# Masked queries on GpSimd in the first attention, and another order of work at the start of the second attention and in the tail

## The chip, the cores and the metric

The kernel runs on one core of one Trainium2 chip, all in fp32. The metric is the device time of one execution in microseconds. The kernel before took 1477.64 us, the median of three runs (1471.13 to 1481.87).

## What is computed

The state x has 64 batch items of 128 rows and 128 features. Two blocks follow each other, each an attention and a feed-forward layer with experts:

```python
x = x + xattn0(layernorm(x), fside, ctx, ctx)        # keys: 128 made from fside, 120 given by ctx
x = x + ffn0(layernorm(x))                           # top 2 of 8 experts, 352 wide, SiLU gate
x = x + xattn1(layernorm(x), ctx, ctx)               # keys: 120 made from ctx
x = x + ffn1(layernorm(x))                           # top 2 of 8 experts of rank 64, GELU, factor 2
```

Both attentions have 16 heads of 8 features: `softmax(q k^T / sqrt(8)) v`, then an output projection with a bias. `q = xn wq + bq`; keys and values are made likewise, and in the first attention the raw context rows are appended to both.

## The kernel before

**Tiling.** A group is four batch items (GB = 4, 16 groups), and an iteration is one item. Groups and items are numbered from 0. With heads of only eight features, the 128 rows of a transposed query tile hold all 16 heads, and a score product uses a strip of 32 rows (`ra`, four of them). To keep the heads that share a strip apart, the query tile is made four times (NS = 4 slots s), each with all features but those of its heads set to zero. That is `q4`, 128 x (4 items, 4 slots, 128 queries). The zeroing is done with a column of `hmask` (128 x 4), the slot's own. In the first attention the scores are taken twice: with queries as rows, to get each row's largest score (`max_bank`, matmul L394, VectorE's reduction L414), and with keys as rows, to get the exponentials in the layout that the product with the values needs (`score_bank`, L430, ScalarE's exp L438). The largest scores are put into unused rows of `q4` by `shift` (transposes L459, VectorE L462), so that L430 subtracts them by itself. In the second attention the largest scores come from an unmasked query tile `qf` (L295) and masked keys `k4`, which `prep_heads` makes with four VectorE multiplications (L313); matmul L407.

**The loop** (L554 on). Iteration `it` takes the largest scores of item `it`, the exponentials of `it - 2`, the product with the values of `it - 3` (L475, `out1` L484), and the output projection of `it - 4` and `it - 5` (L495 to L516). All PSUM tiles are taken from one pool of eight banks (`mtile`, L276). In between, `prep(it, half)` makes what the next group needs, one piece at a time: with j = it % 4, the first attention makes queries at j = 0 (`prep_q`), values and keys at j = 2, and at j = 3 the transposed normed rows `xnT` of the group after it (`prep_x`: four transposes L176 and ScalarE's copy L177). `xnT` has one buffer. `prep_q` is a matmul L292 into a bank, and then ScalarE makes two slots in each half of the iteration: four ACTIVATE L301 a group, each with the slot's column of `bq` as bias and of `hmask` as scale. Group 0 of the first attention is made item by item in `prep_batch`.

**Order.** The code runs under a manual schedule: TensorE, ScalarE, VectorE and GpSimd execute their instructions in the order in which the program issues them, and each waits at the head of its order. GpSimd has the norm of each group (L138 to L146 for mean and root, L167 for the normed rows), the residual's bias (L526), the router's work, and the scatters.

**The router** (class at L625) works on items behind the attention, while it goes on. It is made of generators with due times; `call` is made twice an iteration and takes the pieces that are due: the norm and the logits of a group (`front`; transposes L176, copy L177, products L681), the selection of the two experts of two groups at once (`back`: in the first layer GpSimd's L761, L764, L769 and VectorE's L763 and L768, then in both layers VectorE's small operations on 128x64 elements L718 to L735, and the rows' places L858 to L861), and `sent`, which hands rows out by an indirect transfer from GpSimd (L807) behind a copy of one element (L806) that paces it.

**The second layer.** The experts of the second layer run beside the second attention, in pieces (`Aside1.experts`): the transposed gates (L1420), the first product (L1427) with GELU, the gates spread over the hidden rows (L1439, VectorE L1444), the second product (L1450). `Aside1.rest` (L1469) runs what is left when the attention has ended: one piece, then three router calls, and so on. L740 and L741 are the last operations of the selection, on VectorE and ScalarE.

**Start of the second attention.** Ahead of its loop, the kernel makes the transposed rows (`prep_x(0)`), masked keys (`prep_heads(0)`) and queries (`prep_q(0, 0)`, `prep_q(0, 1)`) of group 0. Group 1 is made in iterations 0 and 1: keys (`prep_k`: matmul L202, ScalarE's L207 twice) and values and rows in 0, queries and masked keys in 1. `loads(1)` issues the transfer of group 1's context rows (L256) just before.

Of the kernel before, what the change touches and what calls it, by code (L numbers as in the profile page):

```python
# [8 lines left out]
F32 = mybir.dt.float32  # L9
I32 = mybir.dt.int32  # L10
AF = mybir.ActivationFunctionType
ALU = mybir.AluOpType
# [6 lines left out]
GB = 4  # L19
NG = B // GB  # L20
S = 128
D = 128
# [22 lines left out]
def transformer_kernel(ctx, tc, a, out):  # L45
    nc = tc.nc
# [185 lines left out]
    def attention(layer, w, norm, first, aside):  # L232
# [5 lines left out]
        with ExitStack() as es:  # L238
# [50 lines left out]
            def prep_q(g, v):  # L289
                if v == 0:  # L290
                    pqs[g] = mtile()
                    nc.tensor.matmul(pqs[g], lhsT=w["wq"], rhs=xnTs[g], start=True, stop=True)  # L292
                pq = pqs[g]
                if v == 0 and not first:
                    nc.scalar.activation(  # L295
                        qfs[g], pq.rearrange("p (b q) -> p b q", b=GB), AF.Identity,
                        bias=w["bqf"],
                    )
                for i in range(2):
                    s = 2 * v + i  # L300
                    nc.scalar.activation(  # L301
                        q4s[g][:, :, s, :], pq.rearrange("p (b q) -> p b q", b=GB),
                        AF.Identity, bias=w["bq"][:, s : s + 1], scale=hmask[:, s : s + 1],
                    )

            def prep_k(g):
                keys_of(w, src[g], g, n0, mtile())

            def prep_heads(g):

                k4s[g] = work.tile([128, NS, GB, KC], F32, name="k4", tag="k4")
                for s in range(NS):
                    nc.vector.tensor_scalar(  # L313
                        k4s[g][:, s], k2[g % 2][:, s // 2], hmask[:, s : s + 1], None, ALU.mult
                    )
# [23 lines left out]
            def prep(it, half):  # L339

                g, j = it // GB + 1, it % GB
                if not first:
                    if g == 1:
                        if (j, half) == (0, 0):
                            prep_k(1)
                            prep_v(1)
                        elif (j, half) == (0, 1):
                            prep_x(1)
                        elif j == 1:
                            prep_q(1, half)  # L350
                            if half:
                                prep_heads(1)
                    elif g < NG:
                        pieces = (
                            (), (lambda: prep_k(g),),
                            (lambda: (prep_heads(g), prep_v(g)), lambda: prep_x(g)),
                            (lambda: prep_q(g, 0), lambda: prep_q(g, 1)),
                        )[j]
                        if half < len(pieces):
                            pieces[half]()  # L360
                    return
                if half == 0 and it < GB - 1:
                    prep_batch(it + 1)
                if (it, half) == (0, 1):
                    prep_v(0)
                    norm_of(1)
                if (it, half) == (1, 1):
                    biased(0)
                if (it, half) == (2, 1):
                    prep_x(1)  # L370
                if (it, half) == (3, 0):
                    prep_q(1, 0)
                    prep_q(1, 1)
                if (j, half) == (3, 1):
                    if g + 1 < NG:
                        prep_x(g + 1)
                elif g >= NG:
                    return
                elif j == 0 and it:
                    prep_q(g, half)  # L380
                elif (j, half) == (2, 0):
                    prep_v(g)
                elif (j, half) == (2, 1):
                    prep_k(g)
# [145 lines left out]
            if first:  # L530
                loads(0)
                yield
                context_k(0)
                yield
                context_v(0)
                loads(1)
                yield
                prep_k(0)
                prep_batch(0)
                yield  # L540
            else:

                ps_[0] = work.tile([128, nc_, 4, 512], F32, name="p", tag="p")
                loads(1)
                for g in range(2):
                    normed[g] = READY[g]
                prep_x(0)
                prep_heads(0)
                prep_q(0, 0)
                prep_q(0, 1)  # L550
            oTs, pos_ = {}, {}
# [745 lines left out]
    aside0 = Aside0()  # L1297
    steps = attention(0, l0, norms[0], True, aside0)
    next(steps)
    l0.update(attention_weights("a0_", ("wq", "bq")))  # L1300
    hmask = load_const("hmask", [128, NS], a["hmask"])
    next(steps)
    l0.update(attention_weights("a0_", ("wv", "bv")))
# [41 lines left out]
    class Aside1:  # L1345
# [122 lines left out]

        def rest(self, mtile):  # L1469
            self.mtile = mtile  # L1470
            while next(self.work, self) is not self:
                for _ in range(3):
                    self.router.call(None, mtile)

    with ExitStack() as es:
# [6 lines left out]
def _laid_out(inp):  # L1482

    import numpy as np

    A = {k: np.asarray(v) for k, v in inp.items()}

    def moved(w):
        w = w.reshape(-1, NV, 4, 2 * HD)[:, ::-1]
        return w.transpose(0, 2, 1, 3).reshape(-1, D)  # L1490

    heads = np.arange(D).reshape(4, NV, 2, HD)
    hm, km, sm = (np.zeros((D, n), np.float32) for n in (NS, NV, NV))
    for v in range(NV):
        km[heads[:, 1 - v].ravel(), v] = 1.0
        sm[np.arange(4) * 32 + 16 * v, v] = 1.0
        for i in range(2):
            hm[heads[:, 1 - v, i].ravel(), 2 * v + i] = 1.0

    o = {"x": A["x"]}  # L1500
    o["fsideT"] = A["fside_BxSxS_0"].transpose(2, 0, 1)
    c = A["ctx_1024"]
    o["ctxT"] = c.transpose(2, 0, 1)
    k = moved(c.reshape(B * KC, D)).reshape(B, KC, 1, D)
    o["ctx_k"] = np.where(km.T > 0, k, sm.T).transpose(3, 2, 0, 1)
    v = np.zeros((B, KC, H // 2, 2, 32), np.float32)
    for i in range(2):
        v[:, :, :, i, 16 * i : 16 * i + HD] = c.reshape(B, KC, H // 2, 2, HD)[:, :, :, i]
        v[:, :, :, i, 16 * i + HD] = 1.0
    o["ctx_v"] = v.reshape(B, KC, H * 32).transpose(1, 0, 2)  # L1510
    o["hmask"], o["kmask"], o["smask"] = hm, km, sm
    for p, l, names, tr in (
        ("a0_", "L0_xattn_", ("Wq", "bq", "Wk", "bk", "Wv", "bv", "Wp", "bp"), False),
        ("a1_", "L1_xattn_", ("W_q", "b_q", "W_k", "b_k", "W_v", "b_v", "W_o", "b_o"), True),
    ):
        wq, bq, wk, bk, wv, bv, wo, bo = (A[l + n] for n in names)
        if tr:
            wq, wk, wv, wo = wq.T, wk.T, wv.T, wo.T
        o[p + "wq"], o[p + "wk"] = moved(wq), moved(wk)
        o[p + "bq"] = np.where(hm > 0, moved(bq).T, np.float32(0.0))  # L1520
        if tr:
            o[p + "bqf"] = moved(bq).T
        o[p + "bk"] = np.where(km > 0, moved(bk).T, sm)
        o[p + "wv"], o[p + "bv"] = wv, bv
        o[p + "wo"], o[p + "bo"] = wo, bo
    o["wqkvT"] = A["L0_ffn_wqkv"].T

    w1 = np.zeros((E, D, 2, NF * 128), np.float32)
    w1[..., :F] = A["L0_ffn_w1"].reshape(E, 2, F, D).transpose(0, 3, 1, 2)
    w2 = np.zeros((E, NF * 128, D), np.float32)  # L1530
    w2[:, :F] = A["L0_ffn_w2"].transpose(0, 2, 1)
    w12 = np.concatenate(
        [w1.reshape(E, D, 2, NF, 128).transpose(0, 1, 3, 2, 4).reshape(E, D, NF, 256),
         w2.reshape(E, NF, 128, D).transpose(0, 2, 1, 3)], axis=3,
    )
    o["w12"] = w12.reshape(E, D, NF * 384)
    o["upper"] = np.triu(np.ones((128, 128), np.float32), 1)
    o["ones"] = np.ones((128, 128), np.float32)
    o["steps256"] = np.arange(CAP // TT, dtype=np.float32) * TT

    t = np.zeros((4, 32, 4, 2, 64), np.float32)
    for e in range(E):
        t[:, e, e // 2, e % 2, :] = 1.0
    o["select"] = t.reshape(128, 4, 128)
    o["tiles"] = np.arange(NA, dtype=np.float32).reshape(1, -1)
    o["row_number"] = np.arange(1, 129, dtype=np.float32).reshape(-1, 1)
    o["first_row"] = np.arange(E, dtype=np.float32) * CAP
    o["wgT"] = A["L1_ffn_Wg"].T
    o["bg"] = A["L1_ffn_bg"]
    o["lw1T"] = A["L1_ffn_W1"].transpose(2, 0, 1).reshape(D, E * R)  # L1550
    o["lw2T"] = A["L1_ffn_W2"].transpose(0, 2, 1).reshape(E * R, D)
    return {k: np.ascontiguousarray(v) for k, v in o.items()}
# [18 lines left out]
```

## Time and profile before

The table is of one profiled execution.

| what | us |
|---|---|
| median of three runs | 1477.64 |
| the profiled execution's own time | 1476.76 |
| its span (first to last instruction) | 1474.9 |
| first attention, loop in its steady part: 60 to 600 us, TensorE busy | 531.13 of 540 |
| routed tiles of the first layer: 600 to 940 us, TensorE busy | 325.86 of 340 |
| start of the second attention: 940 to 1050 us, TensorE busy | 100.61 of 110 |
| second attention, 1050 to 1400 us, TensorE busy | 334.81 of 350 |
| tail, 1400 to 1475 us, TensorE busy | 61.72 of 75 |
| granted TensorE clock, mean over the span | 0.987 of full speed |

How to read the profile: PE is TensorE (PEld its loading of weights), DVE is VectorE, ACT is ScalarE, POOL is GpSimd, SP the engine whose queue issues most transfers; L301 is line 301 of the kernel before. A row of the timeline has its start, its length, engine, line, operation, `output<-inputs` with the tiles' names, and in brackets how long the engine was idle before it and whose result ended that. A row with xN stands for N like instructions close to each other. A row of groups has count, total busy time, mean ns of one, and idle time with its releaser. Ends of matmuls are modelled, so a wait of TensorE inside a stretch can read as busy.

### The profile page before, as it was taken

To read this page: it belongs to the slowest core of one execution; us is meant where nothing else is said; L and a number is where in the kernel's file an instruction comes from. 1 tells how busy PE (TensorE), PEld (TensorE's weight loads), DVE (VectorE), ACT (ScalarE), POOL (GpSimd) and SP (SyncE) were. 2 spreads that over 40 slices of the span, in tenths; PEclk is the share of its full clock that TensorE was granted. 3 is DMA by queue.
4 is the path that set the end of the run, shared out by engine and by line. 5 is a ranking of instruction groups with operands and counts; after the bars stand their busy time and mean duration, and the time that the engine had idled before them with its cause. 6 is when DMAs were issued, how large, how long until landed. Compare 5 with 4: busy or idle time off the path is not lost.

```text
span 1474.9 us, 42033 instructions
## 1 busy us (share of the span) xinstructions
PE 1403.5 (95%) x16620; PEld 1099.4 (75%) x16620; DVE 1111.6 (75%) x3025; ACT 845.2 (57%) x1759; POOL 647.0 (44%) x1195
## 2 busy tenths in 40 slices
PE   7999999999999999999999999898999999999987
PEld 5677777777777777788899998576677677767765
DVE  6777888888888888646574444588988878888863
ACT  3666666666666656643333333466766666766644
POOL 4123346565656554665100131557655666554210
PEclk9999999999999999999999999899999999999999
DMA  8422223333222213247777777301111111110000
GB/s 205 120 77 76 77 77 90 88 92 89 76 64 65 64 44 79 85 141 212 227 215 210 209 215 214 94 28 33 33 30 37 30 40 37 33 30 23 9 16 22
DMA packets 143718, 133.02 MB, mean 90 GB/s; under 512 B 48546, under 2 KB 126114, under 8 KB 141602
## 3 DMA queue, kind: packets, MB, share of 16 engines
q1 hardware_dynamic: 135330, 113.02, 27.9%
q0 software_dynamic: 8192, 17.32, 3.8%
q8 instruction: 132, 2.16, 0.6%
q14 instruction: 64, 0.52, 0.1%
HBM read 97.32 MB, written 32.97 MB: 88 GB/s over the span
## 4 chain that ended last, share of the span: by engine, by line
PE 75%; DVE 17%; POOL 4%; issue 2%; DMA 1%; ACT 1%; SPq 1%; POOLq 0%; DVEq 0%; ACTq 0%
PE bank L430 11%; PE bank L1115 11%; PE bank L394 10%; PE bank L475 9%; DVE nm L414 6%; PE bank L1128 5%; PE bank L1427 4%; PE bank L1450 4%; DVE q L462 2%; PE bank L407 2%; PE bank L214 2%; PE bank L511 2%; PE bank L681 2%; PE bank L202 2%; PE bank L176 2%; PE bank L292 2%
## 5 line engine op out<-in xcount | busy, mean ns | idle before, releaser
L414 DVE TENSOR_REDUCE nm<-bank 128x2 f32<-128x496 f32 (+1 forms) x768 | 463.5, 663 | 82.3 <-PE bank L430 63.2
L438 ACT ACTIVATE p<-bank 120x512 f32<-120x512 f32 (+1 forms) x768 | 402.3, 605 | 130.1 <-PE bank L430 128.4
L430 PE MATMUL bank<-q,k 32*120 32x256 f32 (+1 forms) x3072 | 438.8, 399 | 12.3 <-DVE q L462 5.4
L430 PEld LDWEIGHTS bank<-q,k 32*120 32x120 f32 (+1 forms) x3072 | 294.0, 181 | 51.5 <-DVE nm L414 17.5
L394 PE MATMUL bank<-k,q 32*128 32x248 f32 x2048 | 291.6, 400 | 0.7 <-ACT q L334 0.5
L394 PEld LDWEIGHTS bank<-k,q 32*128 32x128 f32 x2048 | 202.8, 189 | 47.8 <-issue 10.9
L1119 ACT ACTIVATE p<-bank 128x256 f32<-128x256 f32 x213 | 81.0, 384 | 189.3 <-PE bank L1115 189.2
L475 PE MATMUL bank<-p,v 128*32 128x128 f32 (+1 forms) x4096 | 176.2, 276 | 0.3
L1120 DVE TENSOR_TENSOR p<-p,bank 128x256 f32<-128x256 f32 x213 | 86.5, 419 | 89.0 <-ACT p L1119 88.4
L407 PE MATMUL bank<-k,qf 32*128 32x480 f32 x512 | 146.6, 604 | 0.8 <-ACT qf L295 0.8
L807 POOL DMA_INDIRECT xs<-xn,at x128 | 129.6, 1013 | 27.8 <-issue 24.3
L484 ACT COPY ov<-bank 128x256 f32<-128x256 f32 x128 | 48.1, 376 | 142.9 <-PE bank L475 142.9
L475 PEld LDWEIGHTS bank<-p,v 128*32 128x32 f32 (+1 forms) x4096 | 109.3, 110 | 22.7 <-issue 13.8
L1115 PE MATMUL bank<-q 128*128 128x256 f32 x516 | 119.0, 380 | 5.2 <-DMA q<-in_w 3.4
L1367 POOL DMA_INDIRECT yb<-ys,back x112 | 109.0, 973 | 27.7 <-issue 20.9
L167 POOL TENSOR_SCALAR xn<-x,mv,rstd 128x128 f32<-128x128 f32 x252 | 114.3, 465 | 7.1 <-issue 1.0
L462 DVE SCALAR_TENSOR_TENSOR q<-bank,c_smask,q 128x256 f32<-128x256 f32 x256 | 111.1, 476 | 7.2 <-PE bank L459 7.0
L1115 PEld LDWEIGHTS bank<-q 128*128 128x128 f32 x516 | 94.8, 190 | 17.5 <-issue 4.3
L475 PE MATMUL bank<-p,vc 120*32 120x128 f32 x2048 | 103.2, 272 | 0.0
L301 ACT ACTIVATE q<-bank,c_a_bq,c_hmask 128x512 f32<-128x512 f32 x124 | 90.1, 789 | 9.8 <-PE bank L292 9.8
L1157 POOL DMA_INDIRECT kvT<-ys,back x16 | 15.4, 963 | 175.5 <-PE bank L1128 106.4
L138 POOL TENSOR_TENSOR mv<-st 128x4 f32<-128x4 f32 x31 | 6.4, 207 | 196.0 <-DVE st L109 196.0
(227 smaller groups left out, 2469.5 us busy)
## 6 DMA issues: line engine op xcount, KB each, us to landing
q<-in_w SPq DMA_DIRECT2D x43, 576.0 KB, 3.8
vc<-in_w SPq DMA_DIRECT2D x28, 576.0 KB
vc<-in_ctx_v SPq DMA_DIRECT2D x16, 960.0 KB, 7.0
ys<-zero SPq DMA_DIRECT2D x71, 128.0 KB, 1.9
k<-in_ctx_k SPq DMA_DIRECT2D x32, 240.0 KB, 2.8
q<-xs SPq DMA_DIRECT2D x43, 128.0 KB, 2.1
ys<-q SPq DMA_DIRECT2D x43, 128.0 KB, 2.9
x<-in_x SPq DMA_DIRECT2D x16, 256.0 KB, 4.4
```

Source lines behind the costliest of these rows:

```text
L167: nc.gpsimd.tensor_scalar(xn[:, j, :D], xg[g][:, j, :], self.mv[:, b, 0:1], self.rstd[:, b : b + 1], ALU.add, ALU.mult,)
L301: nc.scalar.activation(q4s[g][:, :, s, :], pq.rearrange("p (b q) -> p b q", b=GB), AF.Identity, bias=w["bq"][:, s : s + 1], scale=hmask[:, ...
L394: nc.tensor.matmul(pa[:, u, :], lhsT=q4s[g][r, j, s, :], rhs=k2[g % 2][r, s // 2, j, :], start=True, stop=True,)
L407: lambda: nc.tensor.matmul(pa, lhsT=qfs[g][r, j, :], rhs=k4s[g][r, :, j, :], start=True, stop=True),
L414: nc.vector.tensor_reduce(nm[b % 2].rearrange("q i (a s) -> q a i s", s=16)[:, 2 * ra + v : 2 * ra + v + len(slots) // 2, :, 0], pa.rearra ...
L430: nc.tensor.matmul(pb[:n, v * 256 : (v + 1) * 256], lhsT=k2[g % 2][r, v, j, k0 : k0 + n], rhs=q4s[g][r, j, 2 * v : 2 * v + 2, :].rearrange ...
L438: nc.scalar.activation(ps_[b][:n, c, ra, :], pb[:n], AF.Exp, scale=SCALE)
L462: nc.vector.scalar_tensor_tensor(q, pm, smask[:, v : v + 1], q, ALU.mult, ALU.add)
L475: nc.tensor.matmul(pav[32 * ra : 32 * ra + 32, v * S : (v + 1) * S], lhsT=vs[g % 2][c][:, j, 4 * v + ra, i, :], rhs=p[:n, c, ra, (2 * v + ...
L807: s = nc.gpsimd.indirect_dma_start(xs, bass.IndirectOffsetOnAxis(at[:, j, k : k + 1], 0), xn, None)
L1115: nc.tensor.matmul(ph[:, u, :], lhsT=w[:, c, u * 128 : (u + 1) * 128], rhs=xT, start=True, stop=True)
L1367: nc.gpsimd.indirect_dma_start(y[:, k, b % 2, :], None, ys, bass.IndirectOffsetOnAxis(back[:, b, k : k + 1], 0),)
```

## The change

First attention: for groups 1 to 15, ScalarE makes one unmasked tile of queries with the plain bias `bqf`, and GpSimd makes the four slots from it, two in each call of `prep_q`. The tile takes the buffer of the tag "xnT". `bqf` (128 x 1) is loaded for the first layer too. In the order of the built program, GpSimd's four multiplications follow the scatters of the iteration with j = 0 directly and stand ahead of L138 of the next.

Second attention: the keys of group 1 are made ahead of the loop, before the queries of group 0, and its masked keys in iteration 2 instead of 1; in the built order these four L313 stand behind the VectorE part of `shift` of one item and ahead of the next one's. One exp of a constant is written ahead of all this; it depends on nothing, and in the built program it is ScalarE's first instruction of all.

Tail: the first two pieces in `rest` are followed by no router calls. TensorE's order there becomes L1420, L1427, L1439 of group 13, then L176 and L681 of group 15, then L1450 of group 13.

Lines behind the first edit move by 10 to 15: L313 becomes L323, L394 L404, L414 L424, L430 L440, L438 L448, L475 L485, and so on.

```diff
@@ prep_q
+                if first:
+
+                    if v == 0:
+                        qfs[g] = work.tile([D, GB * S], F32, name="xnT", tag="xnT", bufs=1)
+                        nc.scalar.activation(qfs[g], pq, AF.Identity, bias=w["bqf"])
+                    for s in range(2 * v, 2 * v + 2):
+                        nc.gpsimd.tensor_scalar(
+                            q4s[g][:, :, s, :], qfs[g].rearrange("p (b q) -> p b q", b=GB),
+                            hmask[:, s : s + 1], None, ALU.mult,
+                        )
+                    return
                 for i in range(2):
@@ prep
                         if (j, half) == (0, 0):
-                            prep_k(1)
                             prep_v(1)
                         elif (j, half) == (0, 1):
                             prep_x(1)
                         elif j == 1:
                             prep_q(1, half)
-                            if half:
-                                prep_heads(1)
+                        elif (j, half) == (2, 0):
+                            prep_heads(1)
@@ attention, ahead of the second attention's loop
+                nc.scalar.activation(again[:, 1:2], again[:, 0:1], AF.Exp)
...
                 prep_heads(0)
+                prep_k(1)
                 prep_q(0, 0)
                 prep_q(0, 1)
@@ loading
-    l0.update(attention_weights("a0_", ("wq", "bq")))
+    l0.update(attention_weights("a0_", ("wq", "bq", "bqf")))
@@ Aside1.rest
+            n = 0
             while next(self.work, self) is not self:
-                for _ in range(3):
+
+                n += 1
+                for _ in range(3 if n > 2 else 0):
                     self.router.call(None, mtile)
@@ the host's layout
-        if tr:
-            o[p + "bqf"] = moved(bq).T
+        o[p + "bqf"] = moved(bq).T
```

## The prediction, written before the changed kernel was run

> **What bounds the kernel now.** I read the page from the top: busy time, the chain that ended last, then the group of instructions that the change removes.
>
> ```profile
> PE 1403.5 (95%) x16620; PEld 1099.4 (75%) x16620; DVE 1111.6 (75%) x3025; ACT 845.2 (57%) x1759; POOL 647.0 (44%) x1195
> ...
> PE 75%; DVE 17%; POOL 4%; issue 2%; DMA 1%; ACT 1%; SPq 1%; POOLq 0%; DVEq 0%; ACTq 0%
> ...
> L301 ACT ACTIVATE q<-bank,c_a_bq,c_hmask 128x512 f32<-128x512 f32 x124 | 90.1, 789 | 9.8 <-PE bank L292 9.8
> ```
>
> TensorE is busy 95% of the span, and three quarters of the chain run over it; ScalarE is 57% busy and holds 1% of the chain. By these averages nothing is to be had from ScalarE. The average hides that the first attention has four kinds of iteration, so the next view is the table by stretches, cut at the first `values` matmul (L475) of an iteration: one that makes queries (j = 0), its successor (j = 1), and iteration 60, also j = 0, but with no group left to make queries for.
>
> ```profile
> core 0: us, PE busy (x) PEld busy (x) DVE busy (x) ACT busy (x) POOL busy (x), PEclk, DMA share, GB/s
> 197.12:207.50 10.38, 10.07 (x143) 7.10 (x142) 8.85 (x25) 7.72 (x15) 4.28 (x13) 1.00 0.09 27
> 207.50:216.25 8.75, 8.75 (x144) 7.08 (x143) 7.41 (x22) 5.15 (x11) 6.60 (x17) 1.00 0.35 101
> 575.16:583.35 8.19, 8.19 (x140) 6.56 (x139) 7.99 (x23) 4.95 (x11) 5.65 (x16) 1.00 0.00 0
> ```
>
> Without queries the iteration takes 8.19 us; with them 10.38. The one matmul that is added (L292) runs 1.06. So 10.38 - 8.19 - 1.06 = 1.13 us are a wait, although PE's row reads as busy (ends of matmuls are modelled). Cross-check: j = 1 is 8.75 with four transposes (0.44) that a bare iteration lacks, so 8.31 bare, close to 8.19. VectorE is not the cause: j = 0 keeps its length at 7.7 to 9.2 us of VectorE work. ScalarE has 7.72 us of work, and in ScalarE's timeline two L301 stand ahead of the four exps (L438) of each half:
>
> ```profile
> 200.18 1.45 ACT L301 ACTIVATE q<-bank,c_a_bq,c_hmask 128x512 f32<-128x512 f32 x2 [0.66 <-PE bank L292]
> 201.52 2.29 ACT L438 ACTIVATE p<-bank 120x512 f32<-120x512 f32 x4
> ```
>
> The exps run back to back behind them, up to 1.45 us after their scores, and they free the PSUM banks that TensorE fills next. The second pair of L301 follows at 203.84, and its matmul's result keeps one of eight PSUM banks from 200.2 to 205.3.
>
> **Part 1, masked queries (first attention, groups 1 to 15).** Removed: four L301 a group (784 ns each); added: one ACTIVATE with one pointer (the second attention's L295, the same shape, 690 ns), four GpSimd multiplications. The bank is free after one instruction. Gain: 1.13 us in 14 groups (2 to 15), less 0.3 since iteration 52 has 10.27 us of VectorE work in 11.29: 14 x 1.1 - 0.3 = -15.1 us. Group 1 is made in iteration 3 with GpSimd idle; there the copy L177 of the next group must wait until the four are done with the shared buffer, about when it ran before: 0.
>
> The cost is on GpSimd. The trace has no 128x512 tensor_scalar there. Its nearest row:
>
> ```profile
> L167 POOL TENSOR_SCALAR xn<-x,mv,rstd 128x128 f32<-128x128 f32 x252 | 114.3, 465 | 7.1 <-issue 1.0
> ```
>
> Call one operation x. The timeline sets L167 432 ns apart, and the tensor_scalars of 128x4 (L142 to L144, 199 ns each) 260 ns: 172 ns for 124 more elements, 1.39 ns each, x = 0.26 + 508 x 0.00139 = 0.97. By recorded durations (199 to 451 median) x = 1.24; by straight proportion to L167, 4 x 0.43 = 1.73, an end I give little. Here a rule speaks: the Trainium skill, "GPSIMD Engine Reference", section 3.1 Elementwise, gives 1.8 cycles an element as a good loop with one input (769 ns for 512 elements) and 1.03 as the floor for two operations or fewer, which with the 0.2 us that the small rows cost is an estimated 0.65. L167 at 1.39 ns an element is slower than both. I take 0.90, between 0.97 and the 0.77 of the page, nearer the row; 0.65 and 1.24 stay as ends.
>
> What queues behind them: the four sit in GpSimd's order behind the two scatters of j = 0 and ahead of the norm chain (L138 and on) of j = 1. GpSimd delays TensorE in two ways.
> (a) The port. This trace shows VectorE held up beside GpSimd:
>
> ```profile
> 1024.66 2.68 DVE L313 TENSOR_SCALAR k<-k,c_hmask 128x480 f32<-128x480 f32 x4
> ...
> 1025.76 1.31 POOL L526 TENSOR_TENSOR x<-x,c_a_bo 128x512 f32<-128x512 f32 x1
> ```
>
> The four L313 take 1.60 elsewhere; here one waits about 1 us for the end of L526. VectorE operations that read PSUM (L414, L462) keep their times. That is the rule of the skill's "SBUF — State Buffer", section Who interferes with whom: VectorE's two-input SBUF operations, and its copies and tensor_scalars there, share a port pair with GpSimd exclusively. By the row alone only L313 would be hit, which the first attention has not, and the price would be nothing; by the rule the router's small operations are hit too, and I take the rule. In even groups (iterations 25, 33 .. 57, five of them) the four start at 243.75, and VectorE's L718 to L734 come due at 245.98 - 1.1 = 244.88: 4x - 1.1 us late; then L414, which has 0.77 us to spare, and about 0.3 overlaps with what needs no port: 4x - 2.2 lost. In odd ones (29, 37, 45, 53) the pair L858/L861 meets them the same way.
> (b) Lateness. In odd groups L761 stands behind the norm chain:
>
> ```profile
> 283.85 0.21 POOL L138 TENSOR_TENSOR mv<-st 128x4 f32<-128x4 f32 x1 [2.35 <-DVE st L109]
> ...
> 292.65 1.07 POOL L761 TENSOR_TENSOR pp<-lg 128x512 f32<-128x512 f32 x1
> ...
> 294.92 0.68 DVE L763 TENSOR_REDUCE r<-pp 128x64 f32<-128x512 f32 x1
> ```
>
> GpSimd idles 2.35 us before L138, and L763 starts 1.2 after L761 ends (293.72), so the four may cost 3.55 - 1.1; past that L763 waits, L414 behind it on VectorE, and TensorE for that: 4x - 2.45, not on top of the port's loss in the same group but instead of it. So nine groups lose 4x - 2.2: at 0.90, 9 x 1.4 = +12.6; at 0.65 +3.6; at 1.24 +24.8.
>
> **Part 2, keys of group 1 in the second attention's preamble.** The key matmul L202 is put ahead of the queries' L292, which before ran at 939.73. The keys' transfer is issued at 939.03 and such ones take 2.7 us: L202 runs at 941.5 and L292, L295 and the first scores come up to 1.2 us later. Against that, the four L313 leave this place:
>
> ```profile
> 952.32 1.60 DVE L313 TENSOR_SCALAR k<-k,c_hmask 128x480 f32<-128x480 f32 x4
> ...
> 954.37 0.47 PE L430 MATMUL bank<-q,k 32*120 32x256 f32 x1 [2.06 <-DVE q L462]
> ```
>
> They stood ahead of L462, for which TensorE waits 2.06; L430 gains 1.6 and has lost 1.2. But its exp must load a table first (1.28, at 954.52) and stands behind four L301 that are 1.2 late. Net +1.0 (-0.5 to +2.5). The extra exp written there stands as ScalarE's first instruction of the program, with the table load that came first anyway, and the load at 954.52 stays: 0. The added 128x1 constant delays hmask and the first context keys by about 0.5 us on SP's queue; the keys land near 8 and are needed at 10.6: 0.
>
> **Part 3, tail.** TensorE idles in the last router call:
>
> ```profile
> 1436.54 0.33 PE L176 MATMUL bank<-ident,xn 128*128 128x128 f32 x1 [3.14 <-POOL xn L167]
> ```
>
> Group 13's expert matmuls (L1420, L1427, L1439) are put ahead of it; their gates were ready at about 1422.6. They fill 1433.5 to 1438. Then L681 (before at 1439.03) waits again, about 3 us, since its xnT stands behind group 13's 2.5 us of VectorE and the exp of the router: the output matmuls (L1450) of group 13 come at 1442.5 against 1447.96, and group 14's at 1453.05 against 1457.28, since its gates now come later. The end moves by 1457.28 - 1453.05 = 4.2, less 0.7 for the half clock that PE's rows show in this stretch and that may move onto other matmuls: -3.5 (-1 to -5).
>
> **Sum.** -15.1 + 12.6 + 1.0 + 0 - 3.5 = -5.0. Span 1474.9 becomes 1469.9; the profiled execution (1476.76) has 1.9 around its span: 1471.8; the median of the runs stands 0.9 above that execution: 1472.6, given as 1472.5.
>
> **Rivals.**
> R1, short operations: x = 0.65. The loss is 3.6, the sum -14.0, time 1463.6 (1459 to 1467). For it: the skill's floor, and plain copies here at about 1 ns an element (L823, 64 elements in 241 ns against 177 for one). Against: L167's 1.39.
> R2, the other side: GpSimd takes ScalarE's place. x = 1.24, loss 24.8, sum +7.2, time 1485 (1478 to 1495; the steep end 1.73 would give +25). Place: L718 to L734 and L763 of j = 1 and 2, L414 and TensorE behind them. It decides from 9(4x - 2.2) = 17.6, x = 1.04. For it: recorded durations. Against: the distance between two L167.
> R3, it does not do what it says: the 1.1 us of j = 0 are not ScalarE's but of TensorE's eight banks or VectorE. Then nothing is gained, VectorE comes 1.1 later to meet GpSimd, the loss falls to 9 x 0.3 = 2.7, sum +0.2, time 1478 (1474 to 1483). For it: PE reads as busy 10.07 of 10.38. Against: iteration 60.
>
> **Numbers.** Forecast 0.45 (own range 1467 to 1479), R1 0.20, R2 0.22, R3 0.13. About 1% is what a measurement can tell from no change: bounds 1462.9 and 1492.4. Faster: half of R1 and a little of the forecast, 0.14. Slower: the upper third of R2, 0.08. Same: 0.78. Range 1461 to 1488: it leaves out the fast end of R1 and the upper part of R2.
>
> **What would show it.** Iterations with j = 0 fall from 10.38 towards 9.25 (R3: they don't). The GpSimd rows give x. At j = 1 and 2 L718, L719, L858 lengthen past 0.27, or L763 waits for L761, and L414 with it, in proportion to x. In the second attention L202 starts near 941.5 and the first L430 near 954, with its table load still there. In the tail L1450 starts near 1442.5 and 1453. I am wrong if j = 0 stays, if x lies outside 0.65 to 1.24, or if VectorE's small operations keep their times beside GpSimd.

## The result

The changed kernel takes 1487.07 us, the median of six runs (1485.0 to 1488.91); the kernel before took 1478.68 in six (1471.13 to 1481.87). The ratio is 1.0064 [1.0045, 1.0083]: slower by 0.6%, where 0.35% faster was forecast. The profiled execution took 1485.86, its span 1484.1, 9.2 more than before.

The page of the kernel after, busy time, chain, and the group that is new:

```profile
PE 1397.8 (94%) x16620; PEld 1101.6 (74%) x16620; DVE 1118.9 (75%) x3025; ACT 818.2 (55%) x1715; POOL 737.4 (50%) x1255
...
PE 64%; DVE 20%; POOL 10%; issue 2%; ACT 2%; DMA 1%; SPq 0%; POOLq 0%; DVEq 0%; ACTq 0%
...
L305 POOL TENSOR_SCALAR q<-xnT,c_hmask 128x512 f32<-128x512 f32 x60 | 93.1, 1570 | 20.6 <-ACT xnT L303 20.2
```

TensorE holds 64% of the chain instead of 75%, GpSimd 10% instead of 4%. One multiplication on GpSimd costs 1570 ns, where 900 was taken and 1240 was the upper end (the 1730 of the straight proportion was named and given little). ScalarE has 27 us less to do. The same table by stretches as before, of three iterations after the change: one with j = 0, a j = 1 of an even group, a j = 2 of an odd one:

```profile
core 0: us, PE busy (x) PEld busy (x) DVE busy (x) ACT busy (x) POOL busy (x), PEclk, DMA share, GB/s
197.51:206.75 9.24, 9.24 (x142) 6.85 (x141) 8.35 (x25) 5.84 (x12) 6.82 (x15) 1.00 0.10 30
243.71:253.64 9.93, 9.02 (x144) 7.25 (x143) 9.66 (x24) 5.08 (x11) 9.42 (x16) 1.00 0.30 84
290.21:305.90 15.69, 12.02 (x146) 8.69 (x145) 8.04 (x18) 5.97 (x13) 12.57 (x20) 0.78 0.48 125
```

The last of the three is iteration 30. Before the change it read, in the same columns:

```profile
291.15:301.17 10.02, 9.98 (x147) 7.35 (x146) 8.27 (x19) 5.98 (x13) 8.19 (x12) 1.00 0.62 155
```

The first fell from 10.38 to 9.24, as forecast; the second rose from 8.75, the third from 10.02, with TensorE's granted clock at 0.78 of full speed in it. The whole difference, from the starts of the iterations in the two traces:

| stretch | after minus before, us |
|---|---|
| up to the first iteration with values | +0.3 |
| gain of j = 0, 13 iterations (8 to 56) | -14.8 |
| iterations 3 and 4 (group 1; a stall, then half clock that eats the gain of iteration 4) | +3.5 |
| even groups, j = 1, five iterations (and iteration 53) | +7.1 |
| odd groups, j = 2 (30: 5.68, 38: 5.24, 46: 4.56, 54: 0.23) and iteration 22 (0.91) | +16.6 |
| change to the routed tiles, and the tiles | -0.2 |
| start of the second attention | -1.2 |
| second attention | -0.2 |
| tail | -1.9 |
| sum | +9.2 |

The long odd iteration, in the chain of waits of the kernel after (start, us, what held the chain):

```profile
293.50 0.44 POOL xn L167
...
295.32 1.26 POOL x L536
296.58 1.03 POOL pp L773
297.61 0.02 issue
297.64 0.69 DVE r L775
298.32 0.59 DVE nm L424
298.92 0.04 issue
298.96 0.47 PE bank L514
```

and the same place in the timeline of VectorE and TensorE:

```profile
297.64 0.69 DVE L775 TENSOR_REDUCE r<-pp 128x64 f32<-128x512 f32 x1 [3.58 <-POOL pp L773]
...
298.96 0.47 PE L514 MATMUL bank<-ident,o 128*128 128x128 f32 x1 [3.67 <-DVE nm L424]
299.23 0.64 PE L501 MATMUL bank<-ident,ov 128*128 128x128 f32 x2
299.65 1.96 PE L202 MATMUL bank<-kvT,c_a_wk 128*128 128x512 f32 x2
```

GpSimd is late, VectorE's L775 waits 3.58 us at the head of its order with L424 behind it, and TensorE waits 3.67 for that. Then TensorE runs at half clock: two L202 take 1.96 us, where at this place before the change they took 1.12. The half clock lasts longer in iteration 30 (first line) than in iteration 46 (second line), after the same stall of 3.67:

```profile
298.96:305.00 6.04, 6.04 (x37) 3.85 (x37) 3.40 (x7) 2.80 (x5) 4.48 (x7) 0.50 0.45 134
458.94:462.36 3.42, 3.42 (x33) 2.83 (x32) 1.77 (x5) 2.42 (x4) 3.10 (x5) 0.50 0.39 117
```

So the same stall costs 5.7 us in the one and 4.6 in the other.

### The profile page after: what moved, and what is told of

The parts are those of the page before. It is cut to its first block, busy times and chain, and to the rows that moved or that the text cites. A ratio compares the mean times of both kernels' runs of the same rounds, so it can differ in the third digit from the quotient of the medians.

```text
span 1484.1 us, 42014 instructions
## 1 busy us (share of the span) xinstructions
PE 1397.8 (94%) x16620; PEld 1101.6 (74%) x16620; DVE 1118.9 (75%) x3025; ACT 818.2 (55%) x1715; POOL 737.4 (50%) x1255
## 4 chain that ended last, share of the span: by engine, by line
PE 64%; DVE 20%; POOL 10%; issue 2%; ACT 2%; DMA 1%; SPq 0%; POOLq 0%; DVEq 0%; ACTq 0%
PE bank L1127 11%; DVE nm L424 8%; PE bank L440 8%; PE bank L404 8%; PE bank L485 7%; PE bank L1140 6%; PE bank L1462 4%; PE bank L1439 4%; DVE q L472 3%; POOL xs L819 2%; PE bank L417 2%; POOL q L305 2%; PE bank L202 2%; POOL xn L167 2%; PE bank L214 2%
## 5 line engine op out<-in xcount | busy, mean ns | idle before, releaser
L424 DVE TENSOR_REDUCE nm<-bank 128x2 f32<-128x496 f32 (+1 forms) x768 | 460.5, 661 | 76.6 <-PE bank L440 56.5
L448 ACT ACTIVATE p<-bank 120x512 f32<-120x512 f32 (+1 forms) x768 | 402.5, 603 | 151.1 <-PE bank L440 147.3
L440 PE MATMUL bank<-q,k 32*120 32x256 f32 (+1 forms) x3072 | 436.5, 403 | 11.5 <-DVE lg L697 4.6
L440 PEld LDWEIGHTS bank<-q,k 32*120 32x120 f32 (+1 forms) x3072 | 297.3, 184 | 39.6 <-DVE q L472 9.3
L404 PE MATMUL bank<-k,q 32*128 32x248 f32 x2048 | 291.0, 402 | 1.2 <-ACT q L345 0.5
L404 PEld LDWEIGHTS bank<-k,q 32*128 32x128 f32 x2048 | 208.4, 192 | 54.3 <-issue 17.7
L485 PE MATMUL bank<-p,v 128*32 128x128 f32 (+1 forms) x4096 | 176.5, 276 | 1.9 <-ACT p L448 1.7
L485 PEld LDWEIGHTS bank<-p,v 128*32 128x32 f32 (+1 forms) x4096 | 109.1, 110 | 24.7 <-issue 15.6
L167 POOL TENSOR_SCALAR xn<-x,mv,rstd 128x128 f32<-128x128 f32 x252 | 114.3, 467 | 7.6 <-issue 1.4
L472 DVE SCALAR_TENSOR_TENSOR q<-bank,c_smask,q 128x256 f32<-128x256 f32 x256 | 110.9, 474 | 7.1 <-PE bank L469 6.5
L485 PE MATMUL bank<-p,vc 120*32 120x128 f32 x2048 | 103.9, 274 | 0.0
L305 POOL TENSOR_SCALAR q<-xnT,c_hmask 128x512 f32<-128x512 f32 x60 | 93.1, 1570 | 20.6 <-ACT xnT L303 20.2
L155 POOL TENSOR_SCALAR rstd<-mv 128x4 f32<-128x4 f32 x32 | 6.4, 199 | 189.7 <-DVE mv L113 104.8
```

Source lines behind the costliest of these rows:

```text
L167: nc.gpsimd.tensor_scalar(xn[:, j, :D], xg[g][:, j, :], self.mv[:, b, 0:1], self.rstd[:, b : b + 1], ALU.add, ALU.mult,)
L305: nc.gpsimd.tensor_scalar(q4s[g][:, :, s, :], qfs[g].rearrange("p (b q) -> p b q", b=GB), hmask[:, s : s + 1], None, ALU.mult,)
L404: nc.tensor.matmul(pa[:, u, :], lhsT=q4s[g][r, j, s, :], rhs=k2[g % 2][r, s // 2, j, :], start=True, stop=True,)
L424: nc.vector.tensor_reduce(nm[b % 2].rearrange("q i (a s) -> q a i s", s=16)[:, 2 * ra + v : 2 * ra + v + len(slots) // 2, :, 0], pa.rearra ...
L440: nc.tensor.matmul(pb[:n, v * 256 : (v + 1) * 256], lhsT=k2[g % 2][r, v, j, k0 : k0 + n], rhs=q4s[g][r, j, 2 * v : 2 * v + 2, :].rearrange ...
L448: nc.scalar.activation(ps_[b][:n, c, ra, :], pb[:n], AF.Exp, scale=SCALE)
```

## The experiments

Where a version ran several times, its ratio is to the kernel before on the same chip. On the chips of the first four runs and of the last one under "The changed kernel with the fast form" the kernel before itself took 1545 to 1549 us; only ratios are carried from there.

**Which part loses.** The first part alone (the code of the other two put back), and the other two alone (L301 on ScalarE put back).

> The changed kernel with the second attention's start and the tail put back; only the first attention's queries are changed. Theory A (all that is lost is lost in the first attention, because four GpSimd operations take 6.2 us where 3.5 were free; the other two parts gain a little): the whole loss shows and the small gains go, 11 to 15 us over the kernel before, about 1492. Rival B (the second attention or the tail lost time too, hidden by shifts between stages): at most 9 over, below 1488.

> The changed kernel with ScalarE making the four query tiles as before; start of the second attention and tail stay changed. Theory A: 2 to 5 us under the kernel before, about 1475, of which 1 to 1.5 at the start of the second attention and 1.5 to 2 in the tail. Rival B: no gain or a loss, 1478 to 1482.

Measured: 1486.54 us, 1.0076 [1.0047, 1.0105] for the first part alone; 1474.55, 0.9988 [0.9975, 1.0001] for the rest. The first part's 10 us over before lie between the two ranges that were expected (11 to 15, and at most 9), so the total alone decides nothing. The traces do: all that is lost is lost in the first attention, where the iterations grow and shrink as in the changed kernel (30, 38 and 46 at 14.57 each, there 15.69, 15.25 and 14.57).

**Lateness, the port, or the amount of work.** First, the same four operations at another time, then half of them:

```diff
+                if half and it > 3 and j > 1 and g < NG:
+                    slots(g, j - 2)          # two GpSimd operations at the end of j = 2, two at the end of j = 3
```

> The changed kernel with the four GpSimd operations of a group moved out of j = 0: two stand at the end of j = 2, two at the end of j = 3, from a buffer of their own; group 1 is made by ScalarE as before. Same work on every engine. Theory A (lateness: the norm chain and L773 stand behind the four, and VectorE and TensorE behind L775): j = 0 keeps 9.24, the iterations of 14 to 16 us go back to about 10, and the kernel ends 12 to 17 under the kernel before, about 1464. Rival C (the port: any 6.2 us of GpSimd costs VectorE about the same wherever it stands): 14 groups lose 1.2 or more each, at best 1 us under before, 1478 or more.

> The changed kernel with two of the four query tiles made by GpSimd (in the same place) and two by ScalarE from the bank, groups 2 to 15; group 1 by ScalarE alone. GpSimd has 3.1 us in place of 6.2. Theory A with its threshold (2.45 us may be added before L775 is late): the odd groups' long iterations fall from 14 to 16 us to 10 to 11.5, with no half clock behind them; j = 0 lies between 9.24 and 10.38; about 1470. Rival D (the loss is proportional to GpSimd's time): half of the loss stays, odd groups at 12.5, and the kernel is at about 1479.

Measured: 1465.17 us, 0.9918 [0.9894, 0.9943] with the operations moved, 11 under before, a little less than expected. Every j = 0 takes 9.24, the odd groups' j = 2 are back at 10.02, the even groups' j = 2 have 0.14 more, and from iteration 8 to 64 the first attention takes 507.0 us (before 521.2, changed 530.1). The price of an operation is unchanged, so it was where they stood. With two operations: 1476.18, 0.9998 [0.9985, 1.0012]. Iterations 30, 38 and 46 lose nothing (10.02; 22 still 0.6), so the loss isn't proportional: 3.1 us of GpSimd fit, 6.2 don't. (The prediction's own sum leaves 3.55 free when j = 0 keeps its length, and 2.45 when it is 1.1 shorter.) The total missed the expected 1470, since j = 0 is 10.38 as before: the 1.14 us all hang on the second pair of L301, which this version still has on ScalarE, from the bank.

Then a filler that takes as long but reads nothing (the queries are then a constant), and no GpSimd at all (four L301 from the unmasked tile, one in each half of j = 1 and 2):

```diff
-                        nc.gpsimd.tensor_scalar(q4s[g][:, :, s, :], ..., hmask[:, s : s + 1], None, ALU.mult)
+                        nc.gpsimd.memset(q4s[g].rearrange("p b s q -> p (b s q)")[:, o : o + 1756], 0.05)
```

> The changed kernel with GpSimd's four multiplications replaced by four memsets of 1756 elements, about as long (1.5 us each), which read nothing; the queries of the first attention, groups 1 to 15, are then a constant. If lateness alone makes the odd groups' long iterations, they stay at 14 to 16 us. If VectorE is held up in the even groups by GpSimd's reading, their j = 1 iterations go from 9.94 back to 8.75, and L731, L735, L744, L746 to 0.22; if any GpSimd work holds them up, 9.94 stays.

> The changed kernel with all four query tiles made by ScalarE from the unmasked tile in SBUF, one in each half of the iterations j = 1 and 2, groups 2 to 15; GpSimd has no part in it. If what cost 1.14 us was two L301 in one half iteration ahead of four exps, j = 0 takes 9.24 as with GpSimd, and j = 1 and 2 grow by less than 0.3 each: about 1466, like the version with GpSimd's operations moved. Rival (ScalarE's sum of work counts wherever it stands): j = 1 and 2 grow by about as much as j = 0 lost, 1475.

Measured with fills, 1477.88 us in one run: the odd iterations stay at 15.13 to 15.18, so lateness alone makes them. The even groups' j = 1 go back to 8.75. VectorE's timeline in such an iteration, with the fills:

```profile
242.49 0.23 DVE L731 TENSOR_TENSOR eq<-eq,order 128x64 f32<-128x64 f32 x1
...
243.26 0.84 DVE L744 TENSOR_SCALAR cap<-one 128x64 f32<-128x64 f32 x1
244.13 0.23 DVE L746 TENSOR_TENSOR rest<-r,cap 128x64 f32<-128x64 f32 x1
```

and in the changed kernel, beside the multiplications:

```profile
245.56 0.64 DVE L731 TENSOR_TENSOR eq<-eq,order 128x64 f32<-128x64 f32 x1
...
247.10 0.81 DVE L744 TENSOR_SCALAR cap<-one 128x64 f32<-128x64 f32 x1
247.95 0.66 DVE L746 TENSOR_TENSOR rest<-r,cap 128x64 f32<-128x64 f32 x1
```

Products of two SBUF tiles (L731, L746) are held up beside the multiplications, which read SBUF (0.64 against 0.23), and not beside the fills, which only write; the scaling of one tile (L744) is held up beside either (0.8, alone 0.20). In the changed kernel the five operations that share the port take 1.94 us more than before; 0.77 were to spare, 1.19 is what j = 1 grew by. In the odd groups' j = 1 the fills cost 0.7 that the multiplications don't: casts (L873) of 0.17 take 1.3 to 1.4 beside them.

With ScalarE alone: 1462.37 us, 0.9911 [0.9885, 0.9938]. j = 0 is 9.25, j = 1 unchanged, j = 2 10.08 in every group (before 9.79 and 10.02). ScalarE has about 0.5 us a group more to do than before: the copy takes 0.69, and a tile from SBUF 743 ns where one from the bank took 789. Place and bank are others.

One more version had GpSimd's slow form at the later place, the old start of the second attention and one piece of the tail without router calls. It was expected at about 1464 and took 1461.24 us, 0.9895 [0.9866, 0.9923].

**Place or bank.** Two looks at what those 1.14 us are: ScalarE's four tiles in their old place, but from the unmasked tile in SBUF, and the old L301 from the bank, the second pair half an iteration later:

```diff
+                    for s in range(2 * v, 2 * v + 2):
+                        nc.scalar.activation(q4s[g][:, :, s, :], qfs[g]..., AF.Identity, scale=hmask[:, s : s + 1])
```

```diff
-                    prep_q(g, half)
+                    if half == 0:
+                        prep_q(g, 0)
+                elif (j, half) == (1, 0) and it > 3:
+                    prep_q(g, 1)
```

> The changed kernel with the four query tiles made by ScalarE in their old places (two in each half of j = 0), but from the unmasked tile in SBUF, so that the bank of L292 is free after one instruction; groups 2 to 15. ScalarE has 0.69 us more in the first half. Theory S (the second pair costs 1.14 us because it stands ahead of four exps on ScalarE): j = 0 stays at 10.3 to 10.4, or a little over. Theory K (it costs that because the bank of L292 stays taken until the second pair has run, and the eight banks are taken in turn): j = 0 falls to 9.3 or less, as with GpSimd.

> The changed kernel with ScalarE's L301 as before the change, but the second pair one half iteration later, at the first half of j = 1, groups 2 to 15; the bank of L292 stays taken as much longer. Theory S: j = 0 falls to about 9.24 and j = 1 grows by at most 1.1. Theory K: the bank is missed for the longer, j = 0 and 1 together take more than the 19.1 us of before, by 1 us or more.

Measured, one run of each: 1467.6 us and 1479.04 (before beside them 1476.12). Iteration 24 (j = 0) of each, in the columns of the tables by stretches:

```profile
231.38:241.16 9.78, 9.32 (x142) 6.81 (x141) 8.88 (x22) 7.45 (x16) 6.57 (x17) 1.00 0.12 36
235.49:245.98 10.49, 10.18 (x143) 7.10 (x142) 9.21 (x22) 6.60 (x13) 6.57 (x17) 1.00 0.13 40
```

With the bank free and the place kept, nearly every j = 0 takes 9.78, 0.60 less than before, although ScalarE has about 0.5 us more to do; with the place given up and the bank kept they take 10.48. Neither theory had the sizes right: K expected 9.3 or less in the first version and at least 1 us more for j = 0 and 1 together in the second, where it is 0.1. But S is refuted as the first cause: while the bank is kept, nothing is gained by place. With it free, 0.54 are left to the place and to the copy. Which matmul waits for the bank no trace shows, since PE's rows read as busy.

**Why one operation costs 1.57 us.** A kernel of nothing but operations of GpSimd and VectorE:

> Not the model: operations of GpSimd and VectorE by themselves on tiles of 128 partitions, each four times, and then VectorE's small operations beside a row of GpSimd operations; the output is zeros. What made the query tile cost 1.57 us where 0.90 was taken? Theory P (the price is per element and the same for every tensor_scalar with one input): all tensor_scalars of 512 elements cost 1.5 to 1.6 whether their scale is a column or a number and whether the output is in one piece or four, 256 cost about 0.85 and 128 about 0.5, so 2.8 ns an element. Rival Q (the output in four pieces, or the form with one operation, is what is dear): 512 in one piece or with two operations cost 0.9 to 1.25. Beside GpSimd: VectorE's product of two SBUF tiles (0.2 alone) and its scaling of 64 elements take 0.5 to 0.8 beside tensor_scalars, and about 0.2 beside memsets if GpSimd's reading is what holds them up; reductions keep their times beside both.

Groups of instructions, GpSimd, by form (x count, busy us, mean ns). L44 is the form of the change, L47 the same in one piece, L50 with a number; L53 has two operations with numbers, L56 two with columns:

```profile
L44 POOL TENSOR_SCALAR q<-x,m 128x512 f32<-128x512 f32 x16 | 25.0, 1578 | 3.2 <-DMA x<-in_x 3.2
...
L47 POOL TENSOR_SCALAR y<-x,m 128x512 f32<-128x512 f32 x4 | 6.2, 1562 | 0.3
L50 POOL TENSOR_SCALAR y<-x 128x512 f32<-128x512 f32 x4 | 5.9, 1487 | 0.3
...
L56 POOL TENSOR_SCALAR y<-x,m 128x512 f32<-128x512 f32 x4 | 3.1, 764 | 0.4
L53 POOL TENSOR_SCALAR y<-x 128x512 f32<-128x512 f32 x4 | 2.5, 618 | 0.3
```

Neither theory as it stood: output in four pieces or one is the same (against Q's first half), but the number of operations decides (against P). A tensor_scalar with one operation takes 1.49 to 1.58 us, the same with a second one 0.62 to 0.76, and a copy 0.61. At 256 and 128 elements the slow form takes 0.92 and 0.60. Why the form with one operation is the slow one, no run shows. Beside the slow form VectorE's four products of 64 elements took 1.29 us together, alone and beside fills 1.00; four scalings took 1.69, alone 0.88, beside fills 5.25; reductions from PSUM kept 2.79 for four.

**The changed kernel with the fast form.** One edit, then with the tail's second piece back under the router, then at the later place, then ScalarE's version with the same tail:

```diff
-                            hmask[:, s : s + 1], None, ALU.mult,
+                            hmask[:, s : s + 1], 1.0, ALU.mult, ALU.mult,
...
-                for _ in range(3 if n > 2 else 0):
+                for _ in range(3 if n > 1 else 0):
```

> The changed kernel with one edit: the four GpSimd multiplications are given a second operation that does nothing (times 1.0). By themselves such operations took 0.62 us with numbers and 0.76 with two columns, against 1.56 with one operation. Theory P2 (the form with one operation was the whole mistake in the price; the rest of the working holds): x = 0.65 to 0.75, 4x = 2.6 to 3.0 against 2.4 free, so iterations 30, 38, 46 return to 10.0 to 10.6, the even groups lose at most 0.5, group 1's copy no longer waits, j = 0 stays at 9.24: 13 to 17 us under before, about 1461. Rival (GpSimd is late for L775 by other work than these four, or VectorE is held up by any form): it stays above 1470.

> The same, and in the tail only the first piece without router calls (in the changed kernel two). The tail from the last values product to the end takes about 50.8 as it did so before, against 51.6 to 52.3 with two pieces: 1 us under the run with two operations alone.

> GpSimd's operations at the end of j = 2 and 3, with two operations each, and the tail of one piece. The 0.14 to 0.18 that the even groups' j = 2 still lost with the slow form go away: within 1 us of the run with two operations in the old place and the same tail, about 1460.

> ScalarE's four slots spread over j = 1 and 2, without GpSimd, and the tail of one piece: the even groups' j = 2 keep 0.3 more than with GpSimd, so 1 to 3 us above the two runs with GpSimd's two operations, about 1462.

Measured: 0.9857 [0.9817, 0.9897], 0.9861 [0.9817, 0.9905], 0.9900 [0.9870, 0.9930], 0.9929 [0.9914, 0.9945]. In the first of them an operation takes 696 ns, iterations 30, 38 and 46 are at 10.06 to 10.17, and j = 0 is at 9.24. On this chip some iterations are 0.2 to 1.0 us longer than elsewhere (one by 2.2), with and without GpSimd's part, so the form was run again on another, the first part alone, with all parts, and at the later place:

> The first part alone, as in the first run, with two operations in each GpSimd multiplication. Theory P2: the first attention, iterations 8 to 64, takes 15 us less than with one operation loses, that is 528.4 becomes 508 to 510 (before: 521.2), with even groups at j = 1 at 8.75 to 9.1 and iterations 30, 38, 46 at 10.0 to 10.2: 10 to 15 us under before. Rival (what showed on the slow chip was that chip): iterations 26 and 27 grow by 0.2 to 0.3 here too, and the gain is under 8.

> Two operations, all three parts, one piece of the tail without router calls. If the second attention's start is worth nothing and the tail about 2.5: 2 to 3 us under the run with the first part alone.

> GpSimd's two-operation form at the end of j = 2 and 3, tail of one piece. On the slow chip j = 2 of the even groups grew by 0.7 to 1.0, but by as much without GpSimd, so that growth should be absent here: within 1 us of the version in the old place, since what the old place loses by the port (0.3 in five or six iterations) it does not.

Measured: 1457.61 us, 0.9871 [0.9839, 0.9902]; 1459.55, 0.9880 [0.9849, 0.9910]; 1460.38, 0.9889 [0.9857, 0.9921]. The first part alone went from 1.0076 to 0.9871 by its second operation; from iteration 8 to 64 it takes 506.4 us in place of 528.4. VectorE's timeline of it shows its first router operations in an even group's j = 1, and in iteration 30 the place where L775 waited 3.58 (the line is L774 here):

```profile
238.12 0.78 DVE L729 TENSOR_TENSOR eq<-r,m 128x64 f32<-128x64 f32 x1
238.94 0.62 DVE L730 TENSOR_TENSOR eq<-eq,order 128x64 f32<-128x64 f32 x1
...
286.27 0.69 DVE L774 TENSOR_REDUCE r<-pp 128x64 f32<-128x512 f32 x1 [0.19 <-POOL pp L772]
```

The threshold holds: 2.84 us of GpSimd leave L774 a wait of 0.19, and iteration 30 takes 10.29, 0.28 more than before. In four of the five even groups the port costs 0.28 to 0.34: each of two products (0.22 alone) takes about as long as one GpSimd operation. All this comes to 2.4 us from iteration 8 to 64, and iteration 54, in which TensorE stood still for 2.06 before the change and ran at half clock behind it, is 2.2 shorter. At the later place j = 1 is 8.75, and j = 2 has 0.16 more instead; the totals don't tell the two places apart.

All parts together were expected 2 to 3 us under the first part alone and came out 1.9 over it. The profiled execution had a tail 3.0 us shorter, but iteration 3 was 4.4 longer and the start of the second attention 2.2. So the other two parts gave nothing that these runs can tell (0.9871 against 0.9880).

Last, the fast form and the shorter tail with the old start of the second attention:

> The first part with two operations in each GpSimd multiplication, the tail with its first piece alone free of router calls, and the start of the second attention as before the change. If the parts add up: the first attention's 14.8 us and 2.5 to 3 in the tail (from 53.6 to 50.8 between the last values product and the end), 17 under before, about 1459 where before takes 1476. If the tail's gain is given back elsewhere, 14 to 15 under.

Measured: 0.9822 [0.9795, 0.9850], the best ratio of all, though its interval touches those above. From the last values product to the end it takes 50.80 us, as in four other profiles with one piece free (two more on a chip of 1549 us took 49.5 and 50.0); with two pieces it is 51.6 to 52.3, with none 53.1 to 53.8. The 27 us under before are more than the 17 that the parts sum to. No trace of the kernel before was taken on that chip, so where the rest comes from stays open, and that the tail's gain adds to the first part's is not shown.

## Why the prediction was wrong, step by step

**The 1.13 us of j = 0** were right to 0.01: 10.38 to 9.24 in 12 of the 14 iterations. Iteration 52, from which 0.3 was taken off, gained 1.15 as well; iteration 4 gained nothing behind group 1's stall. The working named two reasons, the place ahead of the exps in each half and the bank, and rested on the first; the runs show the bank in first place (0.60 of the 1.14 with ScalarE's order kept, nothing with the bank kept), and of L301 only the second pair to count, which keeps it. The rival that the banks and not ScalarE's queue set j = 0 was half right, and its conclusion, that nothing would be gained, wrong, since the change frees the bank too. ScalarE's sum of work doesn't count: spread out, it gives j = 0 the same 9.25.

**The price x is the step that failed.** The working took 0.90 from L167, "the nearest row", and 1.24 as the far end. L167 and L142 have two operations, the new instruction one, and that difference, which no row of before shows, is worth 0.81 us (1.57 against 0.76). The page of the Trainium skill that was weighed, "GPSIMD Engine Reference", section 3.1 Elementwise, gives 769 ns for 512 elements with one input; the two-column form measures 764, and the one-operation form twice that. With x as measured and the point from which the sum turns (1.04) the same working would have forecast a slower kernel, by 19 us: the rival in which GpSimd takes ScalarE's place was the case that came, with a still dearer operation. That the rival's 1485 lies so near the measured 1487 is luck, since an operation dearer than its 1.24 and even groups that lost less than it reckoned nearly cancel. Giving the instruction its second operation turned the sign.

**The size of the loss at x = 1.57.** The working's 4x - 2.2 gives 4.1 us a group. Three of the odd groups lost 4.6 to 5.7: the wait (3.6 by the profile, 3.8 by 4x - 2.45) was right, the half clock after it wasn't counted. Even groups lost 1.19, not 4.1: VectorE isn't shut out until GpSimd's four are done, it gets in between them. Late by 1.94, less 0.77 to spare. In the fourth odd group iteration 53 lost 1.2 and iteration 54 only 0.2, since TensorE already stood still and ran at half clock there before. Iteration 22, which the working left out, lost 0.9.

**Group 1** was put at nothing: the copy was to wait for GpSimd's four and still run about when it ran before. With 6.2 us the copy waits 3.94 (here in the kernel after), TensorE after it, and iteration 3 grows by 3.35. Its length varies without that, too: with the fast form iteration 3 took 8.70 us in one profile and 13.14 in another, where TensorE waited 3.06 for the transfer of context keys, and in one with ScalarE making group 1 as before it took 12.90. So the 3.35 are the difference of two executions; what group 1 costs in the mean is not shown.

```profile
43.90 6.20 POOL L305 TENSOR_SCALAR q<-xnT,c_hmask 128x512 f32<-128x512 f32 x4 [11.69 <-ACT xnT L303]
...
50.13 0.59 ACT L177 COPY xnT<-bank 128x512 f32<-128x512 f32 x1 [3.94 <-POOL q L305]
```

**Start of the second attention**, +1.0 forecast, -1.2 in the first profile. From the first transpose to the first values product, in all profiles but those of the first four runs under "The changed kernel with the fast form": old order 20.05 to 21.25 us (five), new order 19.92 to 22.39 (ten). So the -1.2 of the first pair is chance: it has the longest of the old order. The mechanism is as told: in the kernel after the keys' transfer holds L202 for 4.12 us, and TensorE waits for L472 0.80 instead of 2.06.

```profile
954.25 1.94 PE L202 MATMUL bank<-kvT,c_a_wk 128*128 128x480 f32 x2 [4.12 <-DMA kvT<-in_ctxT]
...
965.25 0.47 PE L440 MATMUL bank<-q,k 32*120 32x256 f32 x1 [0.80 <-DVE q L472]
```

What the sum is depends on the clock granted there: with a mean of 0.91 the new order takes 19.9 to 20.1, with 0.76 to 0.77 it takes 21.7 to 22.4, where the old order at 0.75 to 0.76 takes 20.05 to 20.17. Why the clock is granted early in one execution and late in another with the same order stays open. The means (20.9 and 20.3) differ by 0.6, a small loss if anything, within a scatter of 2.5.

**Tail**, -3.5 forecast: -1.5 in the mean (51.6 to 52.3 against 53.1 to 53.8). Counted from the last values product, group 13's output matmuls came 4.8 us earlier, not 5.5, but at half clock (6.10 us for 3.84), and group 14's 1.4 earlier, not 4.2, since TensorE waits 1.99 for its gated rows:

```profile
1452.52 1.88 PE L693 MATMUL bank<-c_wgT,xnT 128*128 128x8 f32 x8 [2.82 <-ACT xnT L177]
1454.25 6.10 PE L1462 MATMUL bank<-c_lw2T,h 128*128 128x128 f32 x32
...
1466.98 3.84 PE L1462 MATMUL bank<-c_lw2T,h 128*128 128x128 f32 x32 [1.99 <-DVE h L1456]
```

With one piece free of router calls the router's copy waits less (1.77 us of TensorE in place of 2.82), and the gain is 2.7.

## What to carry to other kernels

An estimate by the nearest row is only as good as the form of the instruction: before work is moved to another engine, the very form (number of operations, operands, place) is to be priced, since one multiplication on GpSimd cost here 1.57 us or 0.70 by a second operation that does nothing. An engine with much idle time has a slack only up to the next thing that stands in its order: here 2.8 to 3.1 us cost 0.3 or nothing in the odd groups, and 6.2 a stall on two further engines. And a PSUM bank kept for a second reader can cost more than the reading: freed after one copy it gave about half of the gain with ScalarE's own work in the old place, and at j = 0 all of it with that work spread out.

## What was not expected of the hardware

- GpSimd's tensor_scalar with one operation is twice as slow as with two: 1562 against 764 ns with columns, 1487 against 618 with numbers, 512 elements on 128 partitions.
- GpSimd's fill of 1756 elements (1.6 us) holds up VectorE's scalings and casts for up to its own length (0.17 to 1.3 us), but not its products of two SBUF tiles (0.23). The Trainium skill, "SBUF — State Buffer", section Who interferes with whom, says so of both; that beside the slow multiplication VectorE's operations end halfway through GpSimd's (a product of 0.64 within an operation of 1.56) fits it less, while beside the fast form a product took about as long as a whole operation (0.78 and 0.62 beside 0.70).
- The same stall of 3.67 us on TensorE was followed by 3.4 us at half clock in one iteration (46) and by over 6 us in another (30), 1.0 to 2.1 us on top of the stall. What decides between the two, no run shows.
